# Transposes in place of identity products, and first chunks of convolution kernels summed by head selectors

## The chip, the cores and the metric

The kernel runs on one core of one Trainium2 chip. The metric is device microseconds for one launch. Each time given as a median is that of three runs.

## The reference, cut to what matters

Batch and time are 64 x 1024 per head, with 64 heads. For each head a long convolution with a state-space kernel is computed, masked by a length per row; its result feeds a mixture of 64 low-rank experts (rank 16, the best 16 by score, softmax gates), and the sum goes onto x. All is fp32.

```
K = 2.0 * einsum('hn,hnl->hl', Cs, exp(P)).real      # P = dtA * l, 64 states n for each head h
y = irfft(rfft(u_m, 2L) * rfft(K, 2L))[..., :L] + u_m * D[:, None]
y = y * mask
scores = y @ Wr.T ; top 16 of 64 ; gates = softmax(top) ; G = gates at their experts, 0 elsewhere
out = einsum('nkr,kdr->nd', einsum('nd,krd->nkr', y, A) * G, B) * 2
result = x + out
```

## The kernel before, in words

**Tiling.** The 64 heads are eight groups of eight (`HG`), that is four pairs (`GP`); two heads of 64 states fill the 128 partitions. Time is cut into eight chunks of 128. Within a chunk the convolution is a product with a Toeplitz matrix of the kernel's first 128 values (`toep`, 128x128 per head); from chunk to chunk it goes through 64 states per head, which a recurrence on VectorE carries on.

**Stages of a group.** `tables(g)` makes, for each pair, `w` (powers of the state's factor, real and imaginary), `b` (two 128x128 planes on the pair's 128 states: `b[:, 0]` the real terms whose sum over a head's 64 states is the head's kernel, `b[:, 1]` their partner), and `bt`, the same planes with time on the partitions. `conv(g)` then makes the states (`into_states`: `pu` from `x` and `bt`, copied to `s`), runs the recurrence (`recur`), and puts into `pc` the Toeplitz product (`inside`) and the states' part (`across`); VectorE multiplies by the mask into `y`. `gates(g, y)` makes scores: `psh` (two halves of the sum over features, on 2 x 64 partitions), its copy `sh`, then `psc` with tokens on the partitions, then the sixteen best and their softmax in `ex`; `spread_gates` turns `ex` by transposes (`pg`) and sends it through memory. `first(g, ...)` makes the first expert product `h` by the seven products of a Strassen-like scheme; after all groups `second` makes the other expert product (`s`) in the same way.

**Around the change.** In `tables` (L305-L328) each pair's two planes of `b` are turned by products with an identity: L320 moves `identsel`, which is the identity with two columns of head selectors behind it (130 columns), so `pb` gets the turned plane and also, in two columns, the sum over each head's states. L322 turns the other plane. ScalarE copies `pb` to `bt` (L324). `kernels` (L289) adds D (which lies on partition 0 of `d_sb`, zero elsewhere) to those columns on VectorE, giving `kc` with time on the partitions; `rows` (L294) turns `kc` to rows by a product with the identity (L298, `pk`), copies it on ScalarE (`ks`), writes it to `krows` in memory (L301), and reads the Toeplitz tiles back by shifted windows (L302). Group 0 does this in two halves (pairs 0 and 1, issued after pair 2's turn; then pairs 2 and 3), other groups in one. In `gates` each 128 tokens of `sh` are multiplied with `two` (two identities side by side summed, made once at L524), which turns and adds the halves in one (L725); VectorE copies `psc` to `sc` (L729).

**Order.** The work is written as generators: `conv(g)` steps through `tables(g+1)` at set points, and the products `h` of the group before are stepped in between. Most instructions aren't pinned: a planner of the framework gives each engine its order when the kernel is built, from program order, dependencies and modelled costs; at run time each engine follows its fixed order. VectorE keeps program order until the tables of group 0 and the masks are done (`first_order`), ScalarE until the first factor sums are done (`first_copies`), and instructions marked `keep_in_program_order` (the transposes `pg`, transfers, many sums of the last stage) keep theirs. The tables of group 1 are issued after marks of `y`, `ex` and `s` (L1128-L1134). All small PSUM results (`pb`, `pk`, `pu`, `psh`, `psc`, `pg`) share two buffers of one bank each (`ps_k`, tag `pk`); `pc` and `h` have their own. The planes `b` take the places of the tiles `sn` and `k`, which the next table needs. SyncE's queue carries x, `krows`, `toep` and later transfers in order.

Of the kernel before, what the change touches and what calls it, by code (L numbers as in the profile page):

```python
# [37 lines left out]
F32 = mybir.dt.float32  # L38
I32 = mybir.dt.int32
AF = mybir.ActivationFunctionType  # L40
ALU = mybir.AluOpType
AX = mybir.AxisListType
PSUM = bass.MemoryType.PSUM

P = 128
NB = 64
NH = 64
# [3 lines left out]
NE = 64  # L51
# [3 lines left out]
HG = 8  # L55
NG = NH // HG
TOK = HG * NB
NTT = TOK // P
# [4 lines left out]
NP = NH // 2  # L63
GP = HG // 2
NW = P + 1
NCH = NBLK - 1
KROW = P - 1 + P
# [25 lines left out]
def body(ctx: ExitStack, tc, x, xo, lens, par, dvec, at, bm, wt, cst, out):  # L93
    nc = tc.nc
    V = nc.vector
# [5 lines left out]
    def pool(stack, name, bufs, side, **kw):  # L101
        return stack.enter_context(tc.tile_pool(name=name, bufs=bufs, side=side, **kw))
# [5 lines left out]
    ps_k = psum.enter_context(tc.tile_pool(name="ps_k", bufs=2, space=PSUM))  # L108
# [6 lines left out]
    ids = pool(ctx, "ids", 1, "right")  # L115
    const = pool(right, "const", 1, "right")
    xp = pool(right, "xp", 4, "right")
    tp = pool(right, "tp", 1, "right")
    tabp = pool(right, "tabp", 1, "right")
# [8 lines left out]
    cst_sb = ids.tile([P, NW + P + 2 + NBLK], F32, tag="cst", name="cst_sb")  # L128
    nc.scalar.dma_start(cst_sb, cst)
    lens_sb = prep.tile([P, NB], I32, tag="lens", name="lens_sb")  # L130
    d_sb = const.tile([P, NH], F32, tag="dvec", name="d_sb")
    nc.gpsimd.memset(d_sb, 0.0)
    nc.scalar.dma_start(d_sb[0:1, :], dvec)
    lv = cst_sb[:, :NW]
    ident = cst_sb[:, NW : NW + P]
    identsel = cst_sb[:, NW : NW + P + 2]
    feat = cst_sb[:, NW + P + 2 :]
    two = ids.tile([P, NE], F32, tag="two", name="two")

    krows = dram.tile([NH, KROW], F32, tag="krows", name="krows")  # L140

# [97 lines left out]
    def tables(g):  # L239

        j0 = g * GP
        wide = [P, GP, NW]

        def new(t, name=None):
            return tabp.tile(wide, F32, tag=t, name=f"{name or t}_{g}")

        mag, f, k = new("mag"), new("f"), new("k")
        for i in range(GP):  # L250
            nc.scalar.activation(mag[:, i, :], lv, AF.Exp, scale=dt_re[:, j0 + i : j0 + i + 1])
        tt(f, tu_hi[:, j0 : j0 + GP].unsqueeze(2).to_broadcast(wide),
           lv.unsqueeze(1).to_broadcast(wide), ALU.mult)
        yield
        ts(k, f, MAGIC, ALU.add, MAGIC, ALU.subtract)
        yield
        tt(f, f, k, ALU.subtract)
        yield
        for i in range(GP):
            stt(f[:, i, :], lv, tu_lo[:, j0 + i : j0 + i + 1], ALU.mult, f[:, i, :], ALU.add)  # L260
            if i % 2:
                yield
        ts(f, f, HALF_IN, ALU.min, -HALF_IN, ALU.max)

        sh, sn = new("k", "sh"), new("sn")
        nc.scalar.activation(sh, f, AF.Sin, scale=math.pi)
        nc.scalar.activation(sn, f, AF.Sin, scale=2.0 * math.pi)
        nc.scalar.activation(sh, sh, AF.Square)
        nc.scalar.activation(sh, sh, AF.Copy, scale=-2.0, bias=1.0)
        yield  # L270
        w = tab2.tile([P, 2, GP, NW], F32, tag="w", name=f"w_{g}")
        tt(w[:, 1], mag, sn, ALU.mult)
        yield
        tt(w[:, 0], mag, sh, ALU.mult)
        yield
        alpha, nbeta, nalpha = (scales[q] for q in ("alpha", "nbeta", "nalpha"))
        bt = tp.tile([P, GP, 2 * P + 2], F32, tag="bt", name=f"bt_{g}")

        def others():
            return (tab2.tile([P, 3, GP], F32, tag="turn", name=f"turn_{g}"),  # L280
                    tp.tile([P, HG, P], F32, tag="toep", name=f"toep_{g}"))

        if g == 0:
            turn, toep = others()
            tabs[g] = (w, bt, turn, toep)
        kc = tabp.tile([P, HG], F32, tag="kc", name=f"kc_{g}")
        h0 = g * HG

        def kernels(i, n):  # L289

            tt(kc[:, 2 * i : 2 * n].rearrange("p (i a) -> p i a", a=2), bt[:, i:n, 2 * P :],
               d_sb[:, h0 + 2 * i : h0 + 2 * n].rearrange("p (i a) -> p i a", a=2), ALU.add)

        def rows(i, n):  # L294

            w_, row = 2 * (n - i), krows[h0 + 2 * i : h0 + 2 * i + 1, :]
            pk = ps_k.tile([w_, P], F32, tag="pk", name=f"pk_{g}_{i}")
            nc.tensor.matmul(pk, lhsT=kc[:, 2 * i : 2 * n], rhs=ident, start=True, stop=True)  # L298
            ks = tabp.tile([HG, P], F32, tag="ks", name=f"ks_{g}_{i}")[:w_, :]
            nc.scalar.copy(ks, pk)  # L300
            nc.sync.dma_start(krows[h0 + 2 * i : h0 + 2 * n, P - 1 :], ks)  # L301
            nc.sync.dma_start(toep[:, 2 * i : 2 * n, :],  # L302
                              bass.AP(row.tensor, row.offset, [[1, P], [KROW, w_], [1, P]]))

        for i in range(GP):  # L305
            j = j0 + i
            re, im = w[:, 0, i, :P], w[:, 1, i, :P]
            if i % 2 == 0:
                bb = tabp.tile([P, 2, 2, P], F32, tag=("sn", "k")[i // 2], name=f"b_{g}_{i}")
            b = bb[:, i % 2]  # L310
            for c, by in enumerate((alpha, nbeta)):
                if g == 0:
                    ts(b[:, c, :], re, by[:, j : j + 1], ALU.mult)
                else:
                    nc.scalar.activation(b[:, c, :], re, AF.Copy, scale=by[:, j : j + 1])
            stt(b[:, 0, :], im, nbeta[:, j : j + 1], ALU.mult, b[:, 0, :], ALU.add)
            stt(b[:, 1, :], im, nalpha[:, j : j + 1], ALU.mult, b[:, 1, :], ALU.add)

            pb = ps_k.tile([P, 2 * P + 2], F32, tag="pk", name=f"pb_{g}_{i}")
            nc.tensor.matmul(pb[:, P:], lhsT=b[:, 0, :], rhs=identsel, start=True, stop=False,  # L320
                             skip_group_check=True)
            nc.tensor.matmul(pb[:, :P], lhsT=b[:, 1, :], rhs=ident, start=False, stop=True,  # L322
                             skip_group_check=True)
            nc.scalar.copy(bt[:, i, :], pb)  # L324
            if g == 0 and i == 2:
                kernels(0, 2)
                rows(0, 2)
            yield  # L328
        if g:
            turn, toep = others()  # L330
        V.tensor_copy(turn[:, 0:2], w[:, :, :, P])
        ts(turn[:, 2], turn[:, 1], -1.0, ALU.mult)
        if g == 0:
            yield
            kernels(2, GP)
            rows(2, GP)
            return
        kernels(0, GP)
        yield
        rows(0, GP)  # L340
        tabs[g] = (w, bt, turn, toep)


# [4 lines left out]
    def tt(o, a, b, o_):  # L348
        V.tensor_tensor(out=o, in0=a, in1=b, op=o_)  # L349
        return o  # L350

    def ts(o, a, s1, o1, s2=None, o2=None):
        if o2 is None:
            V.tensor_scalar(out=o, in0=a, scalar1=s1, scalar2=None, op0=o1)
        else:
            V.tensor_scalar(out=o, in0=a, scalar1=s1, scalar2=s2, op0=o1, op1=o2)
        return o

    def stt(o, a, s, o1, b, o2):
        V.scalar_tensor_tensor(out=o, in0=a, scalar=s, in1=b, op0=o1, op1=o2)  # L360
        return o
# [43 lines left out]
    s, q = parts  # L405
# [113 lines left out]
    def masks():  # L519
        lens_f = prep.tile([P, NB], F32, tag="lensf", name="lens_f")  # L520
        V.tensor_copy(lens_f, lens_sb)
        tt(mask, feat.unsqueeze(2).to_broadcast([P, NBLK, NB]),
           lens_f.unsqueeze(1).to_broadcast([P, NBLK, NB]), ALU.is_lt)
        tt(two, ident[:, :NE], ident[:, NE:], ALU.add)  # L524

    def right_factors(v, name):

# [182 lines left out]
    def gates(g, y):  # L710
# [3 lines left out]
        for d in range(NBLK):  # L714
# [3 lines left out]
                start=(d < 2), stop=(d >= NBLK - 2),  # L718
            )
        sh = gp.tile([P, TOK], F32, tag="gt", name=f"sh_{g}")  # L720
        nc.scalar.copy(sh, phalf)

        pscore = ps_k.tile([P, NTT, NE], F32, tag="pk", name=f"psc_{g}")
        for t in range(NTT):
            nc.tensor.matmul(  # L725
                pscore[:, t, :], lhsT=sh[:, t * P : (t + 1) * P], rhs=two, start=True, stop=True
            )
        sc = gp.tile([P, NTT, NE], F32, tag="sc", name=f"sc_{g}")
        V.tensor_copy(sc, pscore)  # L729
        m1 = gp.tile([P, NTT, 8], F32, tag="m1", name=f"m1_{g}")  # L730
        m2 = gp.tile([P, NTT, 8], F32, tag="m2", name=f"m2_{g}")
        sa = gp.tile([P, NTT, NE], F32, tag="sa", name=f"sa_{g}")
# [350 lines left out]
    def steps_of(g):  # L1083
        return tables(g) if g < NG else iter(())
# [20 lines left out]
    ahead(products, 1)  # L1105
    for g in range(NG):
        ex = gates(g, y)
        if g:
            spread = {}
# [15 lines left out]
        if g == 0:  # L1125
            tables1, n = steps_of(1), 0
# [50 lines left out]
    n = 0  # L1177
    for _ in products:
# [3 lines left out]
        if n in (5, 6):  # L1182
            i = (1, 6)[n - 5]
# [77 lines left out]
```

## Time and profile before

| | us |
|---|---|
| median of three runs (991.46 to 992.31) | 991.59 |
| the profiled execution | 991.33 |
| its span | 989.5 |
| TensorE busy | 973.5 |
| VectorE busy | 715.6 |
| ScalarE busy | 160.3 |
| GpSimd busy | 332.6 |

The span is what the profile covers; the execution's own time is 1.8 us longer. PE is TensorE's products, PEld its weight loads, DVE is VectorE, ACT ScalarE, POOL GpSimd, SP SyncE. A line number is one of the kernel, but helpers such as `tt` (L349), `ts` (L354, L356) and `stt` (L360) stand for all who call them, so such instructions are told apart by their tiles. A product of TensorE in fp32 shows as two records. The records overlap[...], so the pace of a series is read from starts, or from the pieces of the chain of waits: the list of work that ended last, in order of time, each piece with start, length, engine, tile and line. The wait list says who waited for whom: total, times, longest.

### The profile page before, as it was taken

How to read it: one execution, taken by the hardware profiler on the slowest of the kernel's cores; microseconds unless marked ns; L12 is line 12 of the kernel's file. 1: busy time of each engine (PE TensorE's matmuls, PEld its weight loads, DVE VectorE, ACT ScalarE, POOL GpSimd, SP SyncE). 2: the span in 40 equal slices, each digit the busy share in tenths (PEclk: the TensorE clock that was granted, in tenths of full speed). 3: DMA queues.
4: the chain of work that ended last, by engine and by line, in shares of the span. 5: the costliest groups of instructions: out<-in, count | busy, mean ns of one | idle time of the engine just before them, and what ended most of it. 6: DMA issues, size and time to landing. Idle time of an engine off the chain costs nothing.

```text
span 989.5 us, 12131 instructions
## 1 busy us (share of the span) xinstructions
PE 973.5 (98%) x4394; PEld 733.7 (74%) x4394; DVE 715.6 (72%) x1682; ACT 160.3 (16%) x324; POOL 332.6 (34%) x286
## 2 busy tenths in 40 slices
PE   7899999999999999999999999999999999999998
PEld 3476656676686686676677678888888888888887
DVE  8789699487587587586656749788866785686674
ACT  5245051230231131031001000000000000000000
POOL 0113112023023122113104102255655573754565
PEclk9999999999999999999999999999999999999999
DMA  7825235325315415305315144474574466268432
GB/s 277 208 45 141 93 123 159 107 76 142 125 37 155 139 46 162 136 25 167 136 44 165 67 178 165 161 280 144 202 272 133 146 208 241 87 212 268 136 113 100
DMA packets 67501, 144.01 MB, mean 146 GB/s; under 512 B 9522, under 2 KB 18290, under 8 KB 67442
## 3 DMA queue, kind: packets, MB, share of 16 engines
q1 hardware_dynamic: 49424, 94.40, 28.4%
q0 software_dynamic: 16864, 47.22, 15.3%
q10 hardware_dynamic: 1154, 1.61, 0.6%
q8 instruction: 35, 0.57, 0.2%
q14 instruction: 24, 0.20, 0.1%
HBM read 94.89 MB, written 47.25 MB: 144 GB/s over the span
## 4 chain that ended last, share of the span: by engine, by line
PE 95%; DVE 3%; DMA 1%; issue 0%; POOL 0%; ACT 0%; DVEq 0%
PE h L548 40%; PE s L1030 33%; PE pc L639 6%; PE pc L648 5%; PE pu L613 5%; PE psh L716 3%; PE pb L320 1%; PE psc L725 1%; PE pb L322 1%; DVE hg L349 1%; DMA krows<-ks 0%; PE pg L762 0%; DMA toep<-krows 0%; DVE y L656 0%; PE pk L298 0%; DMA par_sb<-in_par 0%
## 5 line engine op out<-in xcount | busy, mean ns | idle before, releaser
L360 DVE SCALAR_TENSOR_TENSOR s<-s,turn 128x128 f32<-128x128 f32 (+1 forms) x558 | 145.2, 307 | 33.9 <-ACT s L618 27.8
L548 PE MATMUL h<-y,waa 128*128 128x256 f32 x512 | 122.9, 384 | 0.0
L548 PE MATMUL h<-y,was 128*128 128x256 f32 x512 | 117.1, 381 | 0.0
L548 PE MATMUL h<-ty,was 128*128 128x256 f32 x512 | 117.0, 381 | 0.0
L548 PEld LDWEIGHTS h<-y,waa 128*128 128x128 f32 x512 | 93.6, 190 | 27.4 <-issue 16.4
L548 PEld LDWEIGHTS h<-y,was 128*128 128x128 f32 x512 | 96.2, 190 | 19.2 <-issue 6.6
L548 PEld LDWEIGHTS h<-ty,was 128*128 128x128 f32 x512 | 96.5, 190 | 18.1 <-issue 5.4
L800 POOL TENSOR_TENSOR hg<-h_p,gx 128x512 f32<-128x512 f32 x16 | 26.9, 1684 | 222.2 <-DVE h_p L360 213.9
L800 POOL TENSOR_TENSOR hg<-h_u,gx 128x512 f32<-128x512 f32 x32 | 47.7, 1490 | 121.9 <-DVE h_u L349 121.8
L656 DVE TENSOR_TENSOR y<-pc,mask 128x512 f32<-128x512 f32 x64 | 42.4, 685 | 39.4 <-PE pc L648 39.4
L1044 ACT COPY p<-s 128x512 f32<-128x512 f32 x28 | 16.4, 585 | 312.9 <-PE s L1030 301.5
L639 PE MATMUL pc<-x,toep 128*128 128x512 f32 x128 | 61.5, 605 | 1.4 <-DMA toep<-krows 1.4
L897 POOL TENSOR_TENSOR o<-o,acc_a 128x512 f32<-128x512 f32 x32 | 48.1, 1521 | 42.6 <-ACT acc_a L915 32.4
L548 PE MATMUL h<-ty,waa 128*128 128x256 f32 x256 | 58.8, 381 | 0.0
L349 DVE TENSOR_TENSOR hg<-hg 128x512 f32<-128x512 f32 x64 | 42.8, 688 | 21.4 <-POOL hg L800 20.4
L773 POOL DMA_DIRECT2D gx<-gt_dram x56 | 33.7, 631 | 69.0 <-DMA gt_dram<-gt 69.0
L613 PE MATMUL pu<-x,bt 128*64 128x448 f32 x256 | 55.6, 553 | 0.9 <-ACT s L618 0.6
L548 PEld LDWEIGHTS h<-ty,waa 128*128 128x128 f32 x256 | 47.9, 190 | 10.1 <-issue 3.9
L648 PE MATMUL pc<-s,w 64*128 64x448 f32 x248 | 54.7, 561 | 0.0
L618 ACT COPY s<-pu 128x448 f32<-128x448 f32 x62 | 33.0, 532 | 132.2 <-PE pu L613 131.8
L349 DVE TENSOR_TENSOR o<-o,s 128x512 f32<-128x512 f32 (+1 forms) x53 | 35.6, 672 | 25.3 <-PE s L1030 18.2
L897 POOL TENSOR_TENSOR o<-o,b_room 128x512 f32<-128x512 f32 x32 | 50.0, 1582 | 9.8 <-DVE b_room L349 9.8
(234 smaller groups left out, 1610.8 us busy)
## 6 DMA issues: line engine op xcount, KB each, us to landing
x<-in_x SPq DMA_DIRECT2D x32, 512.0 KB
hg_dram<-hg POOLq DMA_DIRECT2D x16, 1024.0 KB, 5.9
o<-in_xo SPq DMA_DIRECT2D x64, 256.0 KB
out<-o SPq DMA_DIRECT2D x63, 256.0 KB
gx<-gt_dram POOLq DMA_DIRECT2D x56, 256.0 KB, 6.1
qy<-hg_dram SPq DMA_DIRECT2D x28, 512.0 KB
r<-hg_dram SPq DMA_DIRECT2D x26, 512.0 KB
hg_dram<-hg POOLq DMA_DIRECT2D x16, 768.0 KB, 4.4
```

What stands on the lines that cost most here:

```text
L349: V.tensor_tensor(out=o, in0=a, in1=b, op=o_)
L360: V.scalar_tensor_tensor(out=o, in0=a, scalar=s, in1=b, op0=o1, op1=o2)
L548: nc.tensor.matmul(bank[:, ii, :], lhsT=fac[n - 1][:, k, (j + ii) * P : (j + ii + 1) * P], rhs=rf[n - 1][:, k, :], start=(first and ii == ...
L613: nc.tensor.matmul(pu[hh * NS : (hh + 1) * NS, :], lhsT=bt[:, i, (1 - c) * P + hh * NS : (1 - c) * P + (hh + 1) * NS], rhs=xt[:, hh, : NCH ...
L618: marks["s"] = nc.scalar.copy(s[:, c], pu.rearrange("p (k b) -> p k b", b=NB))
L639: nc.tensor.matmul(pc, lhsT=toep[:, 2 * i + hh, :], rhs=xt[:, hh, :], start=True, stop=False)
L648: m = nc.tensor.matmul(pcs[hh][:, NB:], lhsT=w[o : o + NS, c, i, 1:], rhs=s[o : o + NS, c].rearrange("p k b -> p (k b)"), start=False, sto ...
L656: marks["y"] = V.tensor_tensor(out=y[:, :, i // 2, 2 * (i % 2) + hh, :], in0=pcs[hh].rearrange("p (k b) -> p k b", b=NB), in1=mask, op=ALU ...
L773: i = queue.dma_start(gx[:, ii, :], gt_dram[g, c * n : (c + 1) * n, :].unsqueeze(1).to_broadcast([n, RANK, TOK]),)
L800: G.tensor_tensor(out=o, in0=a, in1=b, op=op)
L897: tc.keep_in_program_order(G.tensor_tensor(out=o, in0=a, in1=b, op=op_))
L1030: nc.tensor.matmul(bank[:, ii, :], lhsT=left_[i - 1][:, k, ii * P : (ii + 1) * P], rhs=right_[i - 1][:, k, :], start=(first and ii == 0 an ...
```

## The change

The turns of `b` become transposes, two per pair. Groups after the first turn two pairs into one PSUM bank and copy both at once; group 0 copies pair by pair. The sum over each head's states no longer rides on the turn: a product with the two selector columns (`heads`) as the stationary operand and two pairs' `b[:, 0]` as the moving one gives the kernels as rows at once (two heads on two partitions, 256 columns per product). D is added to the first value of each row after the copy, so `d_sb` is 2 x 32. `rows` then only adds D and issues the two transfers; group 0's first half is issued after pair 3's turn, with its products already behind pair 1's turn. `ks` is one tile for the group, of which halves are written. The scores' halves are turned by one transpose per 128 tokens and added by VectorE in the reduction that replaces the copy; `two` is gone.

```diff
-    d_sb = const.tile([P, NH], F32, tag="dvec", name="d_sb")
-    nc.gpsimd.memset(d_sb, 0.0)
-    nc.scalar.dma_start(d_sb[0:1, :], dvec)
+    d_sb = const.tile([2, NP], F32, tag="dvec", name="d_sb")
+    nc.scalar.dma_start(d_sb, dvec)
-    identsel = cst_sb[:, NW : NW + P + 2]
+    heads = cst_sb[:, NW + P : NW + P + 2]
...
-        bt = tp.tile([P, GP, 2 * P + 2], F32, tag="bt", name=f"bt_{g}")
+        bt = tp.tile([P, GP, 2 * P], F32, tag="bt", name=f"bt_{g}")
...
-        def kernels(i, n):
-            tt(kc[:, 2 * i : 2 * n].rearrange("p (i a) -> p i a", a=2), bt[:, i:n, 2 * P :],
-               d_sb[:, h0 + 2 * i : h0 + 2 * n].rearrange("p (i a) -> p i a", a=2), ALU.add)
-        def rows(i, n):
-            w_, row = 2 * (n - i), krows[h0 + 2 * i : h0 + 2 * i + 1, :]
-            pk = ps_k.tile([w_, P], F32, tag="pk", name=f"pk_{g}_{i}")
-            nc.tensor.matmul(pk, lhsT=kc[:, 2 * i : 2 * n], rhs=ident, start=True, stop=True)
-            ks = tabp.tile([HG, P], F32, tag="ks", name=f"ks_{g}_{i}")[:w_, :]
+        all_rows = tabp.tile([2, GP, P], F32, tag="ks", name=f"ks_{g}")
+        def kernels(bbs, i):
+            n = i + 2 * len(bbs)
+            pk = ps_k.tile([2, n - i, P], F32, tag="pk", name=f"pk_{g}_{i}")
+            for m, bb in enumerate(bbs):
+                nc.tensor.matmul(pk[:, 2 * m : 2 * m + 2, :], lhsT=heads, rhs=bb[:, :, 0, :],
+                                 start=True, stop=True)
+            ks = all_rows[:, i:n, :]
             nc.scalar.copy(ks, pk)
-            nc.sync.dma_start(krows[h0 + 2 * i : h0 + 2 * n, P - 1 :], ks)
+            return ks, i, n
+        def rows(ks, i, n):
+            tt(ks[:, :, 0], ks[:, :, 0], d_sb[:, j0 + i : j0 + n], ALU.add)
+            row = krows[h0 + 2 * i : h0 + 2 * i + 1, :]
+            nc.sync.dma_start(
+                krows[h0 + 2 * i : h0 + 2 * n, P - 1 :].rearrange("(i a) l -> a i l", a=2), ks)
             nc.sync.dma_start(toep[:, 2 * i : 2 * n, :],
-                              bass.AP(row.tensor, row.offset, [[1, P], [KROW, w_], [1, P]]))
+                              bass.AP(row.tensor, row.offset, [[1, P], [KROW, 2 * (n - i)], [1, P]]))
...
-            pb = ps_k.tile([P, 2 * P + 2], F32, tag="pk", name=f"pb_{g}_{i}")
-            nc.tensor.matmul(pb[:, P:], lhsT=b[:, 0, :], rhs=identsel, start=True, stop=False,
-                             skip_group_check=True)
-            nc.tensor.matmul(pb[:, :P], lhsT=b[:, 1, :], rhs=ident, start=False, stop=True,
-                             skip_group_check=True)
-            nc.scalar.copy(bt[:, i, :], pb)
-            if g == 0 and i == 2:
-                kernels(0, 2)
-                rows(0, 2)
+            if g == 0 or i % 2 == 0:
+                pb = ps_k.tile([P, 1 if g == 0 else 2, 2 * P], F32, tag="pk", name=f"pb_{g}_{i}")
+            for c in range(2):
+                nc.tensor.transpose(pb[:, i % 2 if g else 0, (1 - c) * P : (2 - c) * P], b[:, c, :], ident)
+            if g == 0:
+                nc.scalar.copy(bt[:, i, :], pb[:, 0])
+            elif i % 2:
+                nc.scalar.copy(bt[:, i - 1 : i + 1, :], pb)
+            if g == 0 and i % 2:
+                halves.append(kernels(bbs[i // 2 :], i - 1))
+            if g == 0 and i == 3:
+                rows(*halves[0])
             yield
...
         if g == 0:
             yield
-            kernels(2, GP)
-            rows(2, GP)
+            rows(*halves[1])
             return
-        kernels(0, GP)
-        yield
-        rows(0, GP)
+        ks = kernels(bbs, 0)
+        yield
+        rows(*ks)
...
-        tt(two, ident[:, :NE], ident[:, NE:], ALU.add)
...
-        pscore = ps_k.tile([P, NTT, NE], F32, tag="pk", name=f"psc_{g}")
+        pscore = ps_k.tile([P, NTT, 2, NE], F32, tag="pk", name=f"psc_{g}")
         for t in range(NTT):
-            nc.tensor.matmul(
-                pscore[:, t, :], lhsT=sh[:, t * P : (t + 1) * P], rhs=two, start=True, stop=True
-            )
+            nc.tensor.transpose(pscore[:, t].rearrange("p s e -> p (s e)"), sh[:, t * P : (t + 1) * P], ident)
         sc = gp.tile([P, NTT, NE], F32, tag="sc", name=f"sc_{g}")
-        V.tensor_copy(sc, pscore)
+        V.tensor_reduce(sc, pscore.rearrange("p t s e -> p t e s"), AX.X, ALU.add)
```

`bbs` collects the tiles `b`, one for two pairs; `halves` what `kernels` returned in group 0.

More of the change, by code (lines that the diff above doesn't have):

```diff
@@ L130, in body @@
     lens_sb = prep.tile([P, NB], I32, tag="lens", name="lens_sb")
-    d_sb = const.tile([P, NH], F32, tag="dvec", name="d_sb")
-    nc.gpsimd.memset(d_sb, 0.0)
-    nc.scalar.dma_start(d_sb[0:1, :], dvec)
+    d_sb = const.tile([2, NP], F32, tag="dvec", name="d_sb")
+    nc.scalar.dma_start(d_sb, dvec)
     lv = cst_sb[:, :NW]
     ident = cst_sb[:, NW : NW + P]
-    identsel = cst_sb[:, NW : NW + P + 2]
+    heads = cst_sb[:, NW + P : NW + P + 2]
     feat = cst_sb[:, NW + P + 2 :]
-    two = ids.tile([P, NE], F32, tag="two", name="two")
     krows = dram.tile([NH, KROW], F32, tag="krows", name="krows")
@@ L285, in tables @@
             tabs[g] = (w, bt, turn, toep)
-        kc = tabp.tile([P, HG], F32, tag="kc", name=f"kc_{g}")
         h0 = g * HG
-        def kernels(i, n):
-            tt(kc[:, 2 * i : 2 * n].rearrange("p (i a) -> p i a", a=2), bt[:, i:n, 2 * P :],
-               d_sb[:, h0 + 2 * i : h0 + 2 * n].rearrange("p (i a) -> p i a", a=2), ALU.add)
-        def rows(i, n):
-            w_, row = 2 * (n - i), krows[h0 + 2 * i : h0 + 2 * i + 1, :]
-            pk = ps_k.tile([w_, P], F32, tag="pk", name=f"pk_{g}_{i}")
-            nc.tensor.matmul(pk, lhsT=kc[:, 2 * i : 2 * n], rhs=ident, start=True, stop=True)
-            ks = tabp.tile([HG, P], F32, tag="ks", name=f"ks_{g}_{i}")[:w_, :]
-            nc.scalar.copy(ks, pk)
-            nc.sync.dma_start(krows[h0 + 2 * i : h0 + 2 * n, P - 1 :], ks)
+        all_rows = tabp.tile([2, GP, P], F32, tag="ks", name=f"ks_{g}")
[6 more added lines that the diff above has]
+            ks = all_rows[:, i:n, :]
+            nc.scalar.copy(ks, pk)
+            return ks, i, n
[4 more added lines that the diff above has]
+                krows[h0 + 2 * i : h0 + 2 * n, P - 1 :].rearrange("(i a) l -> a i l", a=2), ks)
             nc.sync.dma_start(toep[:, 2 * i : 2 * n, :],
-                              bass.AP(row.tensor, row.offset, [[1, P], [KROW, w_], [1, P]]))
+                              bass.AP(row.tensor, row.offset, [[1, P], [KROW, 2 * (n - i)], [1, P]]))
+        bbs, halves = [], []
         for i in range(GP):
@@ L309, in tables @@
                 bb = tabp.tile([P, 2, 2, P], F32, tag=("sn", "k")[i // 2], name=f"b_{g}_{i}")
+                bbs.append(bb)
             b = bb[:, i % 2]
@@ L1238 @@
         "par": par.reshape(5, NP, 2, NS).transpose(2, 3, 0, 1).reshape(P, 5, NP),
-        "dvec": D.reshape(1, NH),
+        "dvec": D.reshape(NP, 2).T,
         "at": A.reshape(NE * RANK, NBLK, P).transpose(2, 1, 0),
```

## Prediction

> **What bounds the kernel now.** I read the page's busy shares and chain first, then a table of busy time by stage, then the chain of waits inside one steady group and at the start, and last what TensorE waited for.
>
> ```profile
> PE 973.5 (98%) x4394; PEld 733.7 (74%) x4394; DVE 715.6 (72%) x1682; ACT 160.3 (16%) x324; POOL 332.6 (34%) x286
> PEclk9999999999999999999999999999999999999999
> ...
> 190.50:267.90 77.40, 77.40 (x352) 53.71 (x352) 54.45 (x158) 17.26 (x36) 17.44 (x18) 1.00 0.35 111
> ```
>
> TensorE is busy 98% of the span, and all 77.40 us of a steady group (the last line: PE, PEld, DVE, ACT, POOL busy, then clock and DMA share). DVE has 23 us to spare in that group. The groups follow each other every 77.44 us (psh starts at 190.48, 267.92, 345.36, 422.80 and 500.24), so from 130 to 575 us a microsecond of TensorE work is a microsecond of time. The clock digit is 9 throughout.
>
> Now the instructions concerned, in the chain of waits of that group (start, length, what):
>
> ```profile
> 187.33 0.42 PE pb L320 x2
> 187.75 0.22 PE pb L322 x2
> 187.97 0.23 PE pb L320 x2
> 188.20 0.22 PE pb L322 x2
> 188.42 0.43 PE h L548 x2
> 188.85 0.22 PE pb L320 x2
> 189.08 0.22 PE pb L322 x2
> 189.30 0.86 PE h L548 x4
> 190.16 0.32 PE pk L298 x2
> ...
> 195.56 0.84 PE psc L725 x8
> 196.40 21.64 PE h L548 x100
> 218.03 0.44 PE pg L762 x4
> ```
>
> Every fp32 product is two instructions (x2), and a pair of 128 columns takes 0.22 us. The existing transposes (pg, four of them) are four instructions, 0.11 us each. A product of 256 columns (h) takes 0.216 us an instruction (21.64/100). That is the price list of the change.
>
> TensorE's own waits:
>
> ```profile
> PE sum L194 <- DMA was<-in_at: 5.3, 1, 5.3
> PE pk L298 <- DVE kc L349: 2.2, 2, 1.5
> PE pc L639 <- DMA toep<-krows: 1.4, 1, 1.4
> ```
>
> The first is the opening load, which nothing here touches. The two others are on the way of the first chunks (kc, pk, ks, krows, toep), which the change rebuilds.
>
> [...]pg has 32 records for 32 calls, median 272 ns each, 0.11 us apart. [...]with four transposes per group the granted clock is 1.00 in every stage. [...]the one here now (den, 256 elements in) takes 0.41 us, as long as the 0.42 us copy of 256, so I price by elements read.
>
> **The change, part by part.** The sum is made against the profiled execution: 991.33 us, of which 989.5 are span; that is 0.26 below the median of 991.59.
>
> *Tables.* Per group, four pairs of products on b (16 instructions) become eight transposes. Old: 1.53 us for the three in the listing (0.42+0.22+0.23+0.22+0.22+0.22) and 0.44 for the first, done earlier at 250.38; 1.97. New: 8 x 0.11 = 0.88, and the 0.20 that the first pair pays after the pc products stays; 1.08. Saved 0.89. A transpose here has 128 stationary columns where pg has 64. From below it is pg's 0.110; from above, psc's loads of 128 columns come every 0.105 (0.84/8), which is no more, so I take 0.11.
>
> *First chunks.* kc is gone, and pk becomes two products with the head selector, 256 columns each: four instructions x 0.216 + 0.10 of entry (0.32 less two at 0.11) = 0.96 against 0.32. Lost 0.64. Bounds: 0.86 without entry, 1.01 at h's slowest pace (3.65/16 = 0.228).
>
> *Scores.* Eight instructions (0.84) become four transposes (0.44). Saved 0.40.
>
> Seven groups have their tables made while TensorE is full: 7 x (0.89 - 0.64) = 1.75. Eight have scores: 8 x 0.40 = 3.2. **Work removed: 4.95 us**, all of it on the bounding engine.
>
> *The wait at 128 us.* The chain there goes through DVE: h_u, a POOL product, four hg, two y, a ty, k, and then kc at 129.46; TensorE stood 1.53 us for kc before pk, with psh queued behind. New: pk needs only b, long done; psh needs y, ready at 127.87. TensorE comes to psh at 125.16 (end of pc) + 0.20 + 6 x 0.11 + 1.29 (six h) + 0.96 = 128.3, later than y. So psh starts at 128.3 and not 129.98: 1.7, of which 0.2 is in the sum above. **Wait removed: 1.5 us** (0 if y comes late too).
>
> *The start.*
>
> ```profile
> 25.86 3.91 DMA krows<-ks
> ...
> 29.79 3.41 DMA toep<-krows
> ...
> 33.24 1.12 PE pc L639 x2
> ```
>
> Here pk sat behind the first pu products and the third pb, so ks was copied only at 25.59, and the two transfers put pc at 33.24. New: pk follows the second b (ready 20.7), its copy is done by about 22.2, and d is added on DVE after the fourth b (22.9); krows can leave near 23.0 and toep be there near 30.4. The second ks copy no longer waits for the first transfer (1.0 us on ACT, with pu behind it), as the halves lie in one tile. TensorE, done with pu at 31.9 now, would be done by some 29.5. So pc could start 2.8 us earlier. DVE sets the next stage: it is 12.80 of 13.20 us busy from 20 to 33.2, and its recurrences and y products run until 43.0 us, before h starts at 43.62. It gains the 1.24 us that it stands at 38.68 for pc, and little else, less perhaps 0.3 because pu waits for a PSUM buffer behind pk. I get pc 2.8 and h about 1.7 earlier. **Start: 1.7 us** (bounds -0.4 and 2.8). The table work saved in group 0 is inside this and counts nothing by itself.
>
> *What I cost at nothing.* DVE: kc goes (0.167 x 9) and `two` (0.22); the small adds take at most kc's 0.167; the score copy (0.42) becomes a sum that reads 512 elements: 0.69 by the y row (128x512 from PSUM), up to 1.3 if the stride of 64 halves the pace. In a steady group ex is ready at 204.9 and pg runs at 218.0, 13 us of cover. In group 0 the cover is 0.5 us (ex 67.15, pg 67.67): there the upper price would cost 0.4. In steady groups the small add waits for ks with DVE's queue behind it, under the same 23 us. The tile k is now freed by pk and not by the last pb, about 1 us later; the next table starts then, and its b is needed 60 us on. ACT: four copies of 0.374 become two of 0.585 (the 128x512 row), ks goes from 0.25 to about 0.58; 17 of 77 us are used. PSUM: from group 1 on one of two buffers is held from the first pb to the second (250 to 265 us), where the program asks for no other. The krows transfer carries the same rows from two partitions instead of eight, with toep queued behind it on SP: steady groups need toep 40 us later; at the start a slower one takes from the 2.8. A memset on POOL goes, at 0.74 us, before anything waits.
>
> Sum: 991.33 - 4.95 - 1.5 - 1.7 = **983.2 us**, 0.8% faster.
>
> **The rivals.** *Only the work counts* (0.22): at the start DVE, already full, gives nothing, and near 128 us the y products come as late as pk did. 991.33 - 4.95 = 986.4. For it: DVE's 97% from 20 to 33 us. Against: 1.24 us of its wait at 38.68 is for pc itself.
> *A new order* (0.10): unpinned instructions are placed by a planner from modelled costs, and shorter instructions move its choices. If TensorE then stands some 0.4 us more in each of seven groups, 2.8 of the gain is lost and the start gives nothing: 989.2; at twice that, no change. Against: h products are at hand as filler at nearly every step.
> *Slower by the clock* (0.04): [...]Against: pg does the same now at a clock of 1.00, and each burst lies among h products.
> *Not single instructions* (0.04): if the fp32 transposes went in two passes after all, tables and scores would save nothing and the selector products would cost 7 x 0.64 = 4.5; with 1.5 and 1.7 gained, 992.6. pg's 32 records for 32 calls speak against it.
>
> **How the numbers follow.** My case has 0.60, from 981 (the start gives 2.8, and the second wait is fully gained) to 985. With the work alone at 986.4 and its spread of 1 us (the price of the selector product and of placing), 0.82 lies within 980.5 to 987.5. A measurement of this kernel can tell about 0.2% (2 us) from no change. Faster by more than that: 0.60 + 0.22 + half of the new orders = 0.87. Within it: 0.05 of new orders and a little of two passes, 0.06. Slower: clock, and two passes with a loss at the start, 0.07.
>
> **What would show it.** The pb group should be 64 records in all (now 128), psc 32 (now 64) and pk 32 (now 18), with starts some 0.22 us apart. The group period should fall from 77.44 to 76.8. The wait of pk for kc should be absent, psh of group 1 should start 1.7 us sooner relative to pc, and the first pc product near 30.5. The granted clock should stay at 1.00. I am wrong if the period doesn't fall, if pc is still at 33, or if TensorE shows a new wait for ACT or for the PSUM buffers.

## The result, and the profile after

| | before | changed |
|---|---|---|
| median, us | 991.50 (six runs, 991.39 to 992.31) | 983.63 (six runs, 983.07 to 984.65) |
| ratio to before | 1 | 0.9921 [0.9908, 0.9934] |
| the profiled execution, us | 991.33 | 983.15 |
| its span, us | 989.5 | 981.3 |

The forecast was 983.2. Of the changed kernel's six executions three lie near 983.2 and one at 984.0, at a mean granted clock of 0.999 or 1.0, and two near 984.6, at 0.997; the last section comes back to them.

From the page of the changed kernel, the busy times and the clock by slices:

```profile
PE 967.1 (99%) x4312; PEld 722.8 (74%) x4312; DVE 717.5 (73%) x1681; ACT 159.7 (16%) x310; POOL 332.3 (34%) x285
...
PEclk9999999999999999999999999999999999999999
```

TensorE has 82 records and 6.4 us less; it is still the bound, with 99% of the span. The clock digit stays at 9. The same steady group as before, in the table of busy time by stage (PE, PEld, DVE, ACT, POOL, then clock and DMA share):

```profile
185.39:262.06 76.67, 76.67 (x342) 52.41 (x344) 54.56 (x157) 17.16 (x34) 17.40 (x18) 1.00 0.37 112
```

It lasts 76.67 us where it took 77.44, all of it TensorE work. Its first part in the chain of waits (start, length, what):

```profile
183.19 0.81 PE pb L326 x6
184.00 0.43 PE h L553 x2
184.43 0.96 PE pk L293 x4
185.39 3.58 PE psh L721 x16
188.97 1.92 PE h L553 x8
190.90 0.44 PE psc L730 x4
191.33 22.02 PE h L553 x102
213.35 0.44 PE pg L765 x4
```

The turns are single instructions (six in 0.81 us, that is 6 x 0.11 and 0.15 of entry, which the first one pays behind the `pc` products), the selector products cost 0.96 and the scores' transposes 0.44. These are the prices of the forecast; only the entry is smaller. Over the whole trace `pb` has 64 records, `psc` 32 and `pk` 32, as forecast. What TensorE waited for (total, times, longest):

```profile
PE sum L192 <- DMA was<-in_at: 4.3, 1, 4.3
PE pg L765 <- DVE sa L755: 1.8, 1, 1.8
...
PE psh L721 <- DVE y L661: 0.9, 2, 0.6
```

The waits for `kc` (2.2 us) and for `toep` (1.4 us) are gone. A wait that I had not forecast is there: `pg` for the gates, 1.8 us, once. It is in group 1 (timeline; the bracket is the idle time ahead and its releaser):

```profile
123.56 3.65 PE L721 MATMUL psh<-y,wt_sb 128*64 128x512 f32 x16 [0.58 <-DVE y L661]
...
136.03 0.42 DVE L755 TENSOR_TENSOR sa<-sa,rd 128x256 f32<-128x256 f32 x1
...
136.60 0.60 PE L765 MATMUL pg<-cst_sb,sa 128*64 128x128 f32 x4 [1.84 <-DVE sa L755]
```

And the start, in the chain of waits:

```profile
20.82 0.59 PE pb L326 x2
21.41 0.52 PE pk L293 x2
21.93 3.29 PE pu L618 x16
...
26.79 3.27 PE pu L618 x16
30.06 3.63 PE pc L644 x8
```

No transfer is in this part of the chain: `pc` starts when `pu` ends, at 30.06, where it waited for `toep` until 33.24. In a second trace of the same kernel it still is ("The changed kernel again" below).

**Where the time came from.** Three marks on TensorE, before and after: the start of `psh` in group 0 goes from 54.09 to 51.10 us (2.99 earlier), in group 2 from 190.48 to 185.39 (5.09), in group 6 from 500.24 to 492.08 (8.16). The span ends 8.2 earlier. Between groups 0 and 2 lies a mark that was better still, group 1: from 129.91 to 123.56 (6.35), of which 1.26 was lost again up to group 2; the wait of `pg` stands there.

### The profile page after: what moved, and what is told of

Its sections match the earlier page's. It is cut to its first block, busy times and chain, and to the rows that moved or that the text cites. A ratio compares the mean times of both kernels' runs of the same rounds, so it can differ in the third digit from the quotient of the medians.

```text
span 981.3 us, 11964 instructions
## 1 busy us (share of the span) xinstructions
PE 967.1 (99%) x4312; PEld 722.8 (74%) x4312; DVE 717.5 (73%) x1681; ACT 159.7 (16%) x310; POOL 332.3 (34%) x285
## 4 chain that ended last, share of the span: by engine, by line
PE 94%; DVE 4%; DMA 0%; issue 0%; POOL 0%; ACT 0%; DVEq 0%
PE h L553 39%; PE s L1033 34%; PE pc L644 6%; PE pu L618 5%; PE pc L653 5%; PE psh L721 3%; PE pb L326 1%; PE pk L293 1%; DVE hg L355 1%; PE pg L765 0%; PE psc L730 0%; DMA par_sb<-in_par 0%; DVE y L661 0%; DVE ty L355 0%; DVE f L366 0%
## 5 line engine op out<-in xcount | busy, mean ns | idle before, releaser
L366 DVE SCALAR_TENSOR_TENSOR s<-s,turn 128x128 f32<-128x128 f32 (+1 forms) x558 | 142.9, 303 | 34.0 <-ACT s L623 28.0
```

## The experiments

My theory after the result had three parts. Work on TensorE fell by 5 to 6 us, in scores and turns, less what the selector products add. The start gave 3.0 because the first rows leave before something that delays them. Near 128 us one wait of 1.5 us went and two others, of 0.6 and 1.8, came. Its rivals: that the scores alone make the steady gain; that the start's gain is the freed `ks` buffer; that it comes from the shorter turns; and that the wait of `pg` is a matter of how much TensorE has to do ahead of it.

**Scores alone**: the kernel before, with the scores' part of the change only.

```diff
-            nc.tensor.matmul(pscore[:, t, :], lhsT=sh[:, t * P : (t + 1) * P], rhs=two, ...)
+            nc.tensor.transpose(pscore[:, t]..., sh[:, t * P : (t + 1) * P], ident)
...
-        V.tensor_copy(sc, pscore)
+        V.tensor_reduce(sc, pscore.rearrange("p t s e -> p t e s"), AX.X, ALU.add)
```

> The kernel before, with only the scores changed (one transpose per 128 tokens, halves added by VectorE in a reduction). Theory 'work on the bounding engine counts one for one': 8 x 0.40 = 3.2 us less, 988.3 us, with the steady group period 0.4 us shorter (77.04). Rival 'the longer reduction on VectorE gives it back': the gates come later, pg waits, as it does for 1.8 us in group 1 of the changed kernel, and the time is 990 or more. The order of TensorE has 20 h products between psc and pg of group 1, as before the change (19), where the changed kernel has 14; so the theory expects no wait of pg here.

Measured: 987.83 us (987.26 to 988.1), ratio 0.9964 [0.9952, 0.9977]. The period, from `psh` at 189.60 to 266.59, is 76.99, which is 0.45 less than before. So the scores are worth 0.45 a group and 3.5 us in all, somewhat under half of the change. Its `pg` waited 0.3 us for the gates, though 40 `h` instructions stood ahead of it where the kernel before has 38: VectorE's new sum takes 0.69 us where the copy took 0.42.

**First chunks alone**: the changed kernel with turns by identity products and scores as before.

```diff
-                nc.tensor.transpose(pb[:, i % 2 if g else 0, (1 - c) * P : (2 - c) * P], b[:, c, :], ident)
+                nc.tensor.matmul(pb[:, i % 2 if g else 0, (1 - c) * P : (2 - c) * P], lhsT=b[:, c, :],
+                                 rhs=ident, start=True, stop=True, skip_group_check=True)
```

> Only the first chunks changed (selector products straight to rows, early in group 0, rows in one tile); turns by identity products of 128 columns, scores as before the change. Theory: the steady groups get 7 x 0.64 = 4.5 us longer, the start gives 3.0 (first pc product near 30 us, first h near 40.6) and the wait for kc near 128 us goes, less some 0.5 of wait for y (1.0): 992.0 us, that is no change in sum. Rival 'only work counts': the start and the wait are other parts' doing, 996.0. Rival 'selector products are hidden': 987.5.

Measured: 991.25 us (991.13 to 991.46), ratio 1.0 [0.9991, 1.0008]. Its chain in the steady group:

```profile
183.99 1.53 PE pb L327 x12
185.53 0.95 PE pk L294 x4
...
191.99 0.84 PE psc L733 x8
```

`psh` starts at 186.48 and again at 264.56: 78.08, so 0.64 more than before. That is the price of the selector products; that it fits to the hundredth is chance, since from start to start `pb` takes 0.10 us more here than in the kernel before and `h` 0.10 less. At the start this kernel has nearly the whole gain (`pc` at 30.23, first `psh` at 51.29), so the gain there belongs to the first chunks and not to the shorter turns. Seven dearer tables (7 x 0.64 = 4.5) eat about what start and `kc` give.

**Turns by products**: the changed kernel with the edit just shown and nothing else.

> The changed kernel, with the turns of b made again by identity products (two instructions of 128 columns each), still two pairs to a copy; scores and first chunks as changed. Theory 'work counts one for one': 7 groups x 8 instructions x 0.11 = 6.2 us more. The order of TensorE has 21 h products ahead of pg in group 1 here, where the changed kernel has 14, so pg's wait of 1.84 us should be absent: 983.6 + 6.2 - 1.8 = 988.0 us, steady period 77.55. Rival 'the turns are hidden among other work': 982 to 984. Rival 'pg's wait comes from the scores' reduction and stays': 989.8.

Measured: 988.06 us (988.01 to 988.08), ratio 0.9966 [0.9952, 0.9979]. The chain:

```profile
183.63 1.53 PE pb L326 x12
185.16 0.95 PE pk L293 x4
```

Twelve records of 1.53 us stand where the transposes are six of 0.81; with the fourth pair, the period is 77.62, which is 0.95 above the changed kernel's. Scores and first chunks add up: 77.44 - 0.45 + 0.64 = 77.63, measured 77.62 in this kernel, which has both. The 0.95 of the turns is the rest, down to 76.67. In this kernel the wait of `pg` is 0.4 us, not 1.8.

**Selector products twice** (groups after the first), which doubles the one cost that the change adds.

```diff
+                for _ in range(2 if g else 1):
                     nc.tensor.matmul(pk[:, 2 * m : 2 * m + 2, :], lhsT=heads, rhs=bb[:, :, 0, :], ...)
```

> The changed kernel with each selector product of groups 1 to 7 issued twice (the second overwrites the first with the same values). Theory 'work counts one for one': 7 x 4 x 0.216 = 6.05 us more; the order has 20 h products ahead of pg in group 1, so its wait of 1.84 goes: 987.8 us, steady period 76.67 + 0.86 = 77.53. Rival 'the selector product lies beside other work': period 76.7, 982 to 984. Rival 'pg's wait stays': 989.7.

Measured: 990.21 us (988.62 to 991.22 in 21 runs), ratio 0.9984 [0.9977, 0.999]. The period is 77.53 (189.18 to 266.71), 0.86 above: four more instructions at 0.215. The wait, though, stayed, as the rival said:

```profile
PE pg L766 <- DVE sa L756: 2.3, 1, 2.3
```

With 40 `h` instructions (20 products) between scores and `pg` where the changed kernel has 28, and VectorE more crowded there, the gates were ready only at 140.4 us. So my simple reading, that more work ahead of `pg` removes the wait, fell: what VectorE has queued at that time counts as well.

**`pg` later**: the changed kernel, with three steps of products instead of two ahead of the spreading of the gates, in group 1 alone.

```diff
-        ahead(products, 1 if g == 0 else 2)
+        ahead(products, 1 if g == 0 else 3 if g == 1 else 2)
```

> The changed kernel, with the gates of group 1 turned and sent one product later in program order (three products of the next stage ahead of them and not two); the order then has 21 h products ahead of pg in group 1 where the changed kernel has 14. Theory 'pg's 1.84 us wait is a matter of its place in TensorE's order': the wait goes, nothing else comes, 981.8 us. Rival 'the gates come late for the sums too': a wait on POOL or VectorE appears in group 1 and the time stays at 983.6. Rival 'the wait only moves to y at the next psh': 983 to 983.6.

Measured: 982.22 us (982.07 to 982.53), ratio 0.9907 [0.9894, 0.9921]; the span is 980.4, so 0.9 shorter than the changed kernel's (the intervals of the two ratios overlap, so that the gain rests on the traces and on the lowest times, 982.1 against 983.0). The wait of `pg` is gone, and most of what it cost stands one step on:

```profile
PE pu L618 <- ACT gt L767: 1.2, 1, 1.2
```

The copy of `pg` on ScalarE now comes behind ScalarE's work for the next table, and `pu` needs its PSUM buffer. So the 1.84 us were a loss of the change of which 0.9 could be had back this way.

**First half's selector products late**: both behind pair 3's turn, in group 0.

```diff
-            if g == 0 and i % 2:
-                halves.append(kernels(bbs[i // 2 :], i - 1))
             if g == 0 and i == 3:
+                halves.append(kernels(bbs[:1], 0))
+                halves.append(kernels(bbs[1:], 2))
                 rows(*halves[0])
```

> The changed kernel, with both selector products of group 0 issued only after pair 3's turn (TensorE then runs the first one behind the four pu products, as before the change), else the same; the order of the rest, the 14 h products ahead of pg in group 1 among it, is that of the changed kernel. Theory 'the early product makes the start': krows leaves near 27 us and not at 22.95, meets the factor transfers, toep comes near 33 and the first pc product with it; 2 to 3 us of the 3.0 of the start are lost, 986 us. Rival 'the one tile for ks and the work saved make the start': pc stays within 0.5 us of 30.0, 984 us.

Measured: 989.31 us (987.91 to 990.99 in 11 runs), ratio 0.998 [0.9971, 0.9989]. The start in its chain:

```profile
26.58 0.15 DVE ks L355
...
26.76 3.23 DMA krows<-ks
...
30.01 3.56 DMA toep<-krows
...
33.61 3.70 PE pc L644 x8
```

The whole start is back: `pc` at 33.61, first `psh` at 54.46. The run doesn't say by what alone, since VectorE stood 3.83 us at the small add, which keeps its place ahead of masks and recurrence. The clock adds to it: this trace has 0.997 in the mean and 0.50 behind the waiting `pg`, though 1.00 behind the wait of 3.7 us for `toep` (last section).

**First rows late**: products as in the changed kernel, add and transfers of the first half moved behind pair 3's step.

```diff
-            if g == 0 and i == 3:
-                rows(*halves[0])
...
         if g == 0:
             yield
+            rows(*halves[0])
             rows(*halves[1])
```

> The changed kernel, with the first half of group 0's rows (the small add and the two transfers) issued only with the second half; the selector products stay early, TensorE's order is unchanged up to that point, and VectorE no longer has the add in its queue ahead of the masks. Theory 'the start is the moment at which krows leaves': it leaves near 27.3 us and not at 22.95, among the factor transfers, toep comes near 34.4 as a transfer of 3.6 and one of 3.4 follow, and the first pc product starts 4.4 us later than at 29.99; psh of group 0 comes 3.5 to 4 us later (51.1 to 54.8) and the time is 987.5. If TensorE's clock falls in the longer wait, up to 2 us more. Rival 'the early selector product and the free pu made the start': pc within 1 us of 30, 984.

Measured: 984.38 us (984.12 to 985.96), ratio 0.993 [0.9917, 0.9944]. The premise failed: the planner put the add at 23.84 all the same, and `krows` left only 1.06 us later than in the changed kernel. What that did is still of use:

```profile
24.01 1.15 DMA krows<-ks
...
25.18 6.08 DMA toep<-krows
...
31.30 3.70 PE pc L643 x8
```

`toep` took 6.08 us and held `pc` for 1.3 us; the first `psh` came at 52.15.

**Two `ks` tiles in the kernel before**, so that the second half's copy doesn't wait for the first half's transfer.

```diff
-            ks = tabp.tile([HG, P], F32, tag="ks", name=f"ks_{g}_{i}")[:w_, :]
+            ks = tabp.tile([HG, P], F32, tag=f"ks{i}", name=f"ks_{g}_{i}")[:w_, :]
```

> The kernel before, with two tiles for ks, so that ScalarE's second copy no longer waits 1.0 us for the first krows transfer and pu is not held behind it. Theory 'toep sets the start': the wait of TensorE moves to toep, the first pc product stays at 33.2 us, 991.5 us. Rival 'the copy's wait was worth a microsecond': pc starts at 32.2 and the time is 990.5.

Measured: 992.69 us (990.98 to 993.49 in 21 runs), ratio 1.001 [1.0003, 1.0016]. `pc` starts at 33.20, as before, after a wait of 2.3 us for `toep`; in the kernel before, the freed buffer gives nothing. Seven executions, at a clock of 0.999 or 1.0, took 991.0 to 991.6, and fourteen, at 0.997 or 0.998, 992.5 to 993.5.

**The changed kernel again**, beside the last ones.

> The changed kernel once more, on the chip of the three others: 983.6 us. pg waits 1.8 us in group 1; in executions in which the granted clock falls behind that wait, about 1.5 us more (984.6 against 983.1).

Measured: 983.04 us (982.97 to 983.64), ratio 0.9915 [0.9901, 0.9928]. The traced execution is the longest of the four, and its start differs from that of the first trace:

```profile
24.11 6.64 DMA toep<-krows
...
30.80 3.70 PE pc L644 x8
```

`krows` left at 22.94 as before, but `toep` landed late enough for TensorE to wait 0.75 us; the first `psh` came at 51.65. So the gain at the start is 2.4 to 3.0 us from one execution to another. `pg` waited its 1.8 us here too, and the clock stayed at 1.00 behind it.

**Sums on VectorE.** The experiments show the selector products as the one dear part (0.64 a group), while VectorE has 22 us to spare in a steady group. So: `pg` later, and from group 3 on VectorE sums the turned planes itself; one transpose of eight columns gives the rows (`d_row` is D as a row on one partition).

```diff
+            V.tensor_reduce(kc.rearrange("p (i a) -> p i a", a=2),
+                            bt[:, :, P:].rearrange("p i (a s) -> p i a s", a=2), AX.X, ALU.add)
+            tt(kc[0:1, :], kc[0:1, :], d_row[:, h0 : h0 + HG], ALU.add)
...
+            nc.tensor.transpose(pk, kc, ident)
```

> The kernel with pg later in group 1, and from group 3 on the sums over a head's states made by VectorE (one reduction of bt, 512 elements in, on a queue with 23 us to spare) and turned by one transpose of 8 columns behind the scores, in place of the selector products. Theory 'TensorE's work is the time': five groups save 0.96 less 0.11 and an entry of 0.10, that is 0.75 each; psh then comes 1.24 us after the pc products and waits some 0.15 for y. Period 76.67 - 0.6 = 76.07, 982.2 - 3.0 = 979.2 us. Rival 'VectorE's queue holds y or the gates back': a wait of psh or pg of over 0.6 us per group, 982 or more.

Measured: 979.54 us (979.37 to 981.08), ratio 0.9882 [0.9868, 0.9895]; period 76.1 (336.22 to 412.32), forecast 76.07.

**The same from group 2 on.**

> As the kernel with VectorE sums, but from group 2 on, whose tables are finished where VectorE is crowded (at 117 to 137 us). Theory 'TensorE's work is the time': 0.6 us less again, 978.6. Rival 'in group 1 VectorE is the bound': the reduction (0.69 us) stands ahead of the gates there, pg or psh waits 0.7 us or more, and the time is that of the other or above: 979.2 to 981.

Measured: 978.05 us (977.97 to 981.44), ratio 0.9872 [0.9858, 0.9885]: the lowest median of all, with an interval that overlaps the one above. Its chain in a steady group:

```profile
257.06 1.28 DVE y L679 x2
...
258.48 3.65 PE psh L739 x16
262.13 2.36 PE h L571 x10
264.49 0.44 PE psc L748 x4
264.92 0.11 PE pk L359
```

The eight columns cost TensorE 0.11 us where the selector products took 0.96, and `pk` no longer stands ahead of `psh`. With so little work left there `psh` waits for `y`: 2.8 us in six waits over the kernel, 1.5 of them in group 1, where group 2's table is finished. So the 0.96 us taken off there gained nothing by itself (that wait was 0.6 in the kernel above), which is the rival's wait, if not its time. Most of the 1.6 us by which the span is shorter than in the kernel above is another thing: the wait of `pu` for the copy of `pg`, 1.2 us there, is absent here. One of the four executions took 981.44 at a clock of 1.0; why is open.

## Why the prediction was right, and where it was not

The total was met to 0.4 us. That it was met so closely is luck: two terms were too small by 0.85 and 1.3 us, one was too large by 0.55, and a wait of 1.84 us was not in the sum at all.

**Work: right in kind, 0.85 us too small.** Forecast 4.95. Measured per group: scores 0.45 (forecast 0.40), turns 0.95 (0.89), selector products +0.64 (0.64); 8 x 0.45 + 7 x (0.95 - 0.64) = 5.8. The turns' 0.05 is the entry: 0.22 + 0.81 = 1.03 us a group in the chain where I had 1.08, against 1.97 before. The scores' 0.05 lies in `h`: from start to start its 224 instructions of a steady group take 49.41 us before and 49.36 with the scores alone changed. Taking a transpose of 128 columns at 0.11 us, from `pg` with 64, was right (among the signs I had written 0.22 between starts, which is the price of `pk` alone).

**Start: the term that was mis-sized most.** Forecast 1.7, measured 2.99 (2.44 in the second trace). I let `pc` gain 2.8 (it gained 3.18), but took VectorE for the bound of the next stage, so that it would pass on little more than the 1.24 us that it stood at 38.68. That step failed. Already in the kernel before, the chain behind `pc` is TensorE's alone, up to `psh` at 54.09:

```profile
33.24 3.70 PE pc L639 x8
36.94 3.21 PE pc L648 x16
40.15 3.63 PE pc L639 x8
43.78 3.45 PE h L548 x16
```

And I had the recurrences and the `y` products of VectorE keep their order. In the changed kernel the planner put 52 instructions of the recurrence ahead of the first `y` product, where before it was 58, and `y` runs at 36.04, where before it came at 38.68:

```profile
22.95 0.31 SPq L303 DMA_DIRECT2D krows<-ks  x1
...
36.04 0.67 DVE L661 TENSOR_TENSOR y<-pc,mask 128x512 f32<-128x512 f32 x1
```

Other kernels show how the first `psh` goes with `pc`:

| | `krows` leaves | its transfer | `pc` starts | first `psh` |
|---|---|---|---|---|
| changed | 22.95 | 1.17 | 30.06 | 51.10 |
| changed, second trace | 22.94 | 1.15 | 30.80 | 51.65 |
| first rows late | 24.01 | 1.15 | 31.30 | 52.15 |
| before | 25.86 | 3.91 | 33.24 | 54.09 |
| selector products late | 26.76 | 3.23 | 33.61 | 54.46 |

The last column is the one before it plus 20.85 to 21.04 in all five: VectorE passed on all that `pc` gained, and was not the bound that I took it for. (With two `ks` tiles it is 22.55, as the clock fell behind that kernel's wait for `toep`, to 0.52 from 34 to 36 us: the first eight `pc` take 5.40 there and 3.70 in the kernel before.) I had also expected the transfer from two partitions to be the same or slower. It took 1.17 us when it left at 22.95 and 3.23, with the same two partitions, when it left at 26.76; so its shape doesn't explain the difference, but the time at which it leaves does. The stretches of "selector products late" show what changes between (DMA share and GB/s are the last two numbers):

```profile
22.00:26.00 4.00, 3.73 (x20) 1.03 (x16) 0.75 (x4) 2.74 (x6) 2.51 (x3) 1.00 0.10 19
26.00:30.00 4.00, 3.94 (x19) 0.96 (x18) 3.38 (x17) 2.37 (x7) 0.29 (x1) 1.00 1.05 178
```

The DMA engines are nearly idle up to 26 us (0.10) and full behind it (1.05). What fills them is GpSimd's queue, on which the expert factors (`was`) are loaded: in the kernel before, where `krows` took 3.91, it moved 0.73 of the 0.74 MB from 26 to 30 us; its loads are issued from 23.01, and the engines fill from 25.2. In "first rows late" they are issued from 23.14, and `krows`, which left at 24.01, still took 1.15. So an early `krows` goes through a gap in front of these loads; that they are what slows the late one fits these traces, but no run moved them. The forecast that `krows` leaves "near 23.0" was right. That the single `ks` tile mattered was not borne out: two tiles gave nothing in the kernel before, and in the changed one the second copy comes long after the first transfer.

**The wait at 128 us: half right.** `kc` and its 1.53 us went. But the sum put six `h` instructions ahead of `psh`, as in the kernel before; the planner placed two. So TensorE came to `psh` before `y` and stood 0.58: 0.95 gained in place of 1.5. That `psh` of group 1 starts 1.9 us sooner behind `pc` (4.75 to 2.84), where 1.7 was forecast, is so only because four `h` instructions were put off. "0 if `y` comes late too" was the right bound to have written.

**What I did not foresee: `pg` in group 1, 1.84 us.** I gave the cover of `pg` in a steady group (13 us) and in group 0 (0.5 us), and not in group 1. There it was nothing: the kernel before runs 38 `h` instructions from `psc` to `pg`, and stands 0.12 us:

```profile
135.46 8.26 PE h L548 x38
```

In the changed kernel 28 stand there (6.2 us), while VectorE needs 7.9 us from the end of `psc` (128.6) to the end of `sa` (136.45), 1.2 of them for instructions of the next table (`f`) that stand ahead of the scores' sum. The rival "a new order" had this mechanism, at 0.4 us in each of seven groups; it came once, at 1.84. Why the planner placed fewer products there is open.

The sum as measured: 2.99 + 5.8 + 0.95 - 1.84 = 7.9 of 8.2 us; most of the rest lies between the first `psh` of group 0 and that of group 1, where `h` and `pu` take 0.6 us less for the same number of instructions, from start to start. Fewer entries like the 0.15 above could do that; no run tested it.

**What I costed at nothing.** The scores' sum on VectorE, priced by elements read after the reduction `den`, takes 0.69 us (L732), the lower of the two prices that I gave and as long as a `y` product (0.68), which reads 512 elements too; the stride of 64 adds nothing to that. The small add takes 0.15 and the double copies 0.59. TensorE shows no wait for ACT over 0.3 us.

**The rivals.** "Only the work counts" (986.4) fell with the start. "Not single instructions" fell with the records. "Slower by the clock", that is by a clock that the transposes lower, fell too: every steady group, with sixteen transposes, has 1.00. Where the clock did cost time (1.7 us by the estimate of the last section), it was behind a stand of TensorE, which I had not considered.

## What to carry to other kernels

Where one engine is full, count its instructions by the pace in the chain of waits: three such prices gave the period to 0.12 us in 77. Look up each wait that has little cover in the group where the cover is least, group 1 here, since a planner may place less work there as soon as one stage gets shorter. Before an engine is called the bound of a stage, look whether it is in the chain of waits there: VectorE was 97% busy at the start and was not. And once the full engine is relieved, look at what the change added to it: a sum of 0.96 us moved to VectorE, which had time, took 0.55 us off each steady group (76.67 to 76.12).

## What the runs showed of the hardware

A stand of TensorE costs more than its length, in some executions. In the profiled execution of "first rows late", `pg` of group 1 waits the same 1.8 us as in the changed kernel, and the clock (the number before the last two) falls behind it:

```profile
136.00:138.00 2.00, 0.36 (x4) 0.36 (x4) 1.86 (x6) 1.99 (x3) 0.00 (x0) 1.00 0.00 0
138.00:140.00 2.00, 2.00 (x9) 0.70 (x6) 1.39 (x3) 1.81 (x4) 0.00 (x0) 0.75 0.00 0
140.00:142.00 2.00, 2.00 (x6) 0.39 (x5) 0.00 (x0) 0.00 (x0) 0.57 (x1) 0.50 0.29 66
142.00:144.00 2.00, 2.00 (x8) 1.14 (x10) 1.37 (x5) 1.07 (x2) 2.00 (x5) 0.90 0.45 150
```

TensorE is busy 0.36 of the first 2 us; then, as an estimate from these clocks, 2 x (0.25 + 0.50 + 0.10) = 1.7 us are lost. The kernel with two `ks` tiles shows the same behind its 2.3 us for `toep`:

```profile
34.00:36.00 2.00, 2.00 (x4) 0.75 (x3) 2.00 (x10) 0.08 (x1) 0.42 (x2) 0.52 0.17 49
36.00:38.00 2.00, 2.00 (x4) 0.79 (x3) 1.48 (x7) 0.00 (x0) 1.40 (x2) 0.62 0.29 90
```

In "first rows late", too, the executions at 0.997 (985.7 and 986.0) are about 1.6 us above the others (984.1 to 984.4, at 0.999 or 1.0); with selector products twice the two places are 988.6 to 989.1 and 990.2 to 991.2. But the length of a stand doesn't decide by itself. In the traces of the changed kernel the same 1.8 us leave the clock at 1.00, and so does the longest of these stands, that of "selector products late", where TensorE waits 3.7 us for `toep` up to 33.6:

```profile
34.00:36.00 2.00, 2.00 (x6) 0.90 (x5) 2.00 (x10) 0.00 (x0) 0.73 (x1) 1.00 0.14 43
```

In the same execution the clock falls behind the 1.8 us of `pg`, to 0.77, 0.50 and 0.88 in three stretches of 2 us (140 to 146). With selector products twice it is 0.63 and 0.52 (140 to 144) behind the 2.3 us of `pg`. The estimate of above gives 1.7 us lost in each of these four falls. So a stand of 1.8 us was enough in two traces, and one of 3.7 us cost no clock; what decides is not shown by any run. The wait of `pg` takes 1.8 us in both traces of the changed kernel, and probably some 1.5 more in the executions at 984.6, whose clock of 0.997 fits (an estimate, 984.6 against 983.1); no trace of such an execution was taken, so the place is inferred. In the four executions of "`pg` later", without that wait, the clock stayed at 1.0.
